# Pacing the density of the last image but one, with one product on ScalarE and its sum on GpSimd

## The chip, the core and the metric

The kernel runs on one core of a Trainium2 chip. A core has five engines with instruction queues of their own, each worked off in order: TensorE (PE: matrix products; its weight loads are listed as PEld), VectorE (DVE: elementwise work and reductions), ScalarE (ACT: activation functions with a scale and a bias), GpSimd (POOL) and SyncE (SP: here only DMA issues). The metric is the device time of one execution in microseconds (us), as the median of several runs.

## The reference

The input x has 8 images of 192 channels and 64 x 64 points. Two layers follow each other:

```
x = x + attention(group_norm(x))
x = x + density(group_norm(x))

attention: q = prelu(w1 x), k = prelu(w2 x) (24 channels), v = prelu(wa x) (192 channels)
           out = softmax(q' k over 4096 points) v
density:   l = xr - 0.5 and l = xr + 0.5, each through four small layers per channel:
             l = softplus(m_i) l + b_i          (1 -> 3 -> 3 -> 3 -> 1 values)
             l = l + tanh(f_i) * tanh(l)        (not after the last)
           likelihood = max(|sigmoid(s upper) - sigmoid(s lower)|, 1e-6), s = -sign(lower + upper)
```

So attention is matrix work and one exp per score, and the density is a long chain of products, sums and tanhs on every point, once for the lower and once for the upper side.

## The kernel before, in words

**Steps.** The attention is worked off in steps: per image 8 rows of queries (512 each), per row 16 steps (`STEPS`), so 128 steps per image (`IMG`) and 1024 in all (`last`). In step t PE makes the scores of step t + 1 (line 896, two matmuls), the scores for the row maximum of step t + 25 (line 825, `LEAD` = 25), and the products of step t with the values (line 912, eight matmuls). ScalarE takes the exp (line 901), DVE the row maximum (line 833). The last 25 steps have no maximum to make. At the end of a row, ScalarE scales the sums (line 936), PE turns them (line 946), DVE adds them to x (line 957) and takes the norm's statistics (line 516). Beside this the next image's norm, keys and values are prepared; the last image (number 7) has none of that. The row maximum has one PSUM buffer (`ps_mx`), the scores for the exp one (`ps_sc`), and exp's result two.

**Units.** The density of image b starts when its attention is done, so it runs beside the attention of image b + 1, and image 7's runs alone behind the last step (the tail). It is cut into 12 units per image: a half of the points (c), a third of the channels (g), and a side (s, lower or upper). A unit works on tiles of 128 x 1024 from a pool of 17 buffers. For the images 0 to 6 a unit is, in its written order:
- ScalarE: three first tanhs (line 1158, `tanh0`); three products of the first of them by a scale (line 1167, `begin`), to each of which GpSimd issues a DMA that adds x (line 1172);
- DVE: six products with sum (line 1186 through `mix`), two for each of the three layer values, namely with the second and with the third first tanh; behind each pair ScalarE's second tanh (line 1180);
- DVE: three gates, then six operations for the next layer, with a third round of tanhs on ScalarE, three gates, and one operation for the last layer; the last product of that layer is already made on ScalarE (line 1222, `plain`) and summed by GpSimd in two halves (line 1228).

Image 7's units make their first layer on PE: `product` (line 1125) sums x and three tanhs in PSUM for each of the three values, with a bank filled by ScalarE (line 1109, `fill`) where one was used before; ScalarE takes the tanh from there (line 1134) and DVE the first gate (line 1144).

**Endings.** When both sides of a pair are done, `ending` makes the likelihood. Where it begins before step `last - 12` the sum, difference and product go to GpSimd as pieces of half a tile (lines 1416, 1429, 1437); from there on, `alone` makes them on DVE (lines 1449, 1464, 1465). The store into x is DVE's (line 1479) in both.

**GpSimd's pieces.** A queue, `pieces`, gives out one piece per step (`pool_step`), each behind a small memset (line 1377, `pause`) that waits for the last DVE operation but one of the density, so that the piece lies beside the row maximum, which reads PSUM.

**The planner.** The order on each engine is written at build time. A step's fixed work and what is due (`due`, `run_due`) come first, then `density_step` lets units give out operations as long as they have credit. DVE's credit per step is a rate: the operations left in this image, times their cost, over the steps until a due step, plus 0.1, at most 3.1 (`MOST`). The due step is b * 128 + 271 for image b's density, and step 1032 within the last 25 steps, with a cap of 4.1 there. `Unit.step` takes an operation only if what it needs was given out in an earlier step (for DVE, only tanhs and the DMA's sums have to be earlier), if buffers are left, and if the step's cost stays below `FULL`. Behind the last step `tail_step` takes over: it keeps a clock per engine, gives each operation a duration, and gives out the one that could start first. Nothing at run time looks at these costs; only the order is left, with its waits.

`zs`, `bufs`, `norms` (scales and biases of the image's norm), `xc` (the image being added to) and `at(t, fn, cost...)` (run fn in step t) are used by all of them.

Of the kernel before, what the change touches and what calls it, by code (L numbers as in the profile page):

```python
# [11 lines left out]
AF = mybir.ActivationFunctionType  # L12
# [6 lines left out]
def kernel(  # L19
# [35 lines left out]
    F = 512  # L55
# [336 lines left out]
    def at(t, fn, cost=0.0, act=0.0, pe=0.0):  # L392

        due.setdefault(max(t, now[0]), []).append((fn, cost, act, pe))
# [617 lines left out]
            banks.append(t)  # L1012
    zs = {}

    class Unit:

        def __init__(self, b, c, g, s):
            self.key = b, c, g, s  # L1020
            self.at = {}
            self.done = {}
            self.buf = {}
            self.todo = {"DVE": deque(), "ACT": deque(), "PE": deque()}
            self.left = {"l": 6, "t": 9, "u": 0, "z": 1, "p": 1}
            self.held = {"l": 0, "t": 0, "u": 0, "z": 0, "p": 0}
            self.on_pe = b == B - 1
            add = self.add
            if self.on_pe:

                self.left.update(t=3, u=3, p=0)
                for i in range(3):
                    add("ACT", ("u", 0, i), [], self.tanh0, makes="u")
                for i in range(3):
                    after = [("u", 0, j) for j in range(3)]
                    if i:

                        add("ACT", ("fill", i), [("sum", 0)], self.fill)
                        after.append(("fill", i))
                    add(  # L1040
                        "PE", ("sum", i), after, self.product,
                        frees=[("u", 0, j) for j in range(3)] if i == 2 else [],
                    )
                    if i:
                        add("ACT", ("l", 1, i - 1), [("sum", i - 1)], self.tanh1, makes="l")
                add("ACT", ("l", 1, 2), [("sum", 2)], self.tanh1, makes="l")
                for i in range(3):
                    add("DVE", ("gate", 1, i), [("l", 1, i)], self.gate1)
            else:
                for i in range(3):  # L1050
                    add("ACT", ("t", 0, i), [], self.tanh0, makes="t")
                    if i == 0:
                        for k in range(3):
                            add(
                                "ACT", ("l", 1, k), [("t", 0, 0)], self.begin, makes="l",
                                frees=[("t", 0, 0)] if k == 2 else [],
                            )
                for i in range(3):
                    for j in (1, 2):
                        add(  # L1060
                            "DVE", ("mix", i, j), [("t", 0, j), ("x", i)], self.mix,
                            frees=[("t", 0, j)] if i == 2 else [],
                        )
                    add("ACT", ("t", 1, i), [("mix", i, 2)], self.tanh, makes="t")
                for i in range(3):
                    add("DVE", ("gate", 1, i), [("t", 1, i)], self.gate, frees=[("t", 1, i)])
            for i in range(3):
                add("DVE", ("l", 2, i), [("gate", 1, 1)], self.two, makes="l")
                add("DVE", ("add", 2, i), [("gate", 1, 2), ("gate", 1, 1)], self.third)
# [93 lines left out]
        def begin(self, k):  # L1163
            b, c, g, s = self.key
            i = k[2]
            dst, x_ = self.buf[k], self.src()
            nc.scalar.activation(  # L1167
                dst, self.buf["t", 0, 0], AF.Copy, scale=norms[b, 1][1][:, g, 3 * i : 3 * i + 1]
            )

            def add():
                nc.gpsimd.dma_start(out=dst, in_=x_, accum_op=ALU.add)  # L1172
                self.at["x", i] = now[0] + 1

            at(now[0] + 1, add)

        def tanh(self, k):
            b, c, g, s = self.key
# [113 lines left out]
        def step(self, eng, t, older):  # L1292
            todo = self.todo[eng]
            while todo and credit[eng] > 0:
                name, after, fn, makes, frees = todo[0]
                if any(self.at.get(a, t) >= t for a in after if eng != "DVE" or a[0] in "tux"):
                    return
                if makes and len(bufs) <= sum(u.need() for u in older) + len(endings):
                    return
                cost = COST[eng]  # L1300
                if spent[eng] + cost > FULL[eng] - max(0.0, late[eng] - 0.7):
                    return
                todo.popleft()
# [31 lines left out]
    def density_step(t, rate):  # L1335
        if t >= last:
            return tail_step(t)
        if units:

            left = sum(len(u.todo["DVE"]) for u in units if u.key[0] == units[0].key[0])  # L1340
            rate = left * COST["DVE"] / max(1, (units[0].key[0] + 2) * IMG + 15 - t) + OTHER
            rate = min(rate, MOST)
            if t + LEAD >= last:

                rate = min(left * COST["DVE"] / (last + 8 - t) + OTHER, MOST + 1.0)

        for eng, most in (("DVE", rate), ("ACT", ACT_RATE)):
            credit[eng] = min(credit[eng] + most, most + 1.3)
        for eng in ("ACT", "DVE"):
            order = list(range(min(3, len(units))))  # L1350
            if len(units) == 2:

                order.sort(key=lambda n: -len(units[n].todo["DVE"]))
            for n in order:
                units[n].step(eng, t, list(units)[:n])
        for u in [u for u in units if not u.busy()]:
            units.remove(u)
# [345 lines left out]
```

## Time and profile before

| | |
|---|---|
| median of 3 runs | 4351.46 us (4350.76 to 4351.48) |
| the profiled execution | 4350.1 us, span 4348.1 us |
| granted TensorE clock | 0.986 |
| PE, DVE, ACT, POOL busy | 4217.4, 3883.2, 2848.1, 1118.2 us |
| end of the last step (last L912) | 4050.0 us from the span's start |
| image 6's rows of steps, image 7's rows | 499.1, 461.2 us |

The page gives the busy time of each engine, the chain of work that ended last, and the costliest groups of instructions, each with its line, engine, operation, tiles (out<-in, buffer numbers left out), count, busy time, mean duration and the idle time ahead of it. The windows view gives, for each stretch of the span, the busy time of each engine in us with the number of its instructions, the granted clock, and the share and rate of the DMA engines. The timeline lists instructions in the order of time with their start, duration, and in brackets the engine's idle time before and what ended it; equal ones that follow each other are merged (x3). Starts are us from the span's start. A DVE operation's duration overlaps the next one's start by some 0.1 us, so the distance of starts is what one costs.

### The profile page before, as it was taken

Reading aid. Unit: us, or ns where it says so; the run is one execution under the profiler, and the core shown is the slowest. Engines: PE = TensorE matmul, PEld = TensorE weight load, DVE = VectorE, ACT = ScalarE, POOL = GpSimd, SP = SyncE. Lnnn points to the kernel's source line nnn. Section 1 sums busy time; section 2 is a strip of 40 time slices with the busy share of each in tenths; the row PEclk is TensorE's granted clock in tenths of the full one; section 3 lists DMA queues with packets and bytes.
Section 4 is the critical chain, followed back from the end, with each engine's and each line's share of the span. In section 5 each row is a group of like instructions: output and inputs, shape, how many; then the busy total and the mean of one; then the engine's idle time right before and its main releaser. Section 6 shows DMA issues by size and latency. Waiting matters only on the chain.

```text
span 4348.1 us, 59628 instructions
## 1 busy us (share of the span) xinstructions
PE 4217.4 (97%) x23464; PEld 3810.4 (88%) x23464; DVE 3883.2 (89%) x4055; ACT 2848.1 (66%) x3104; POOL 1118.2 (26%) x1204
## 2 busy tenths in 40 slices
PE   7999999999999999999999999999999999999796
PEld 4999999999999999999999999999999998999432
DVE  5444359999999998999999999999999999999999
ACT  1333337776777767677677767777677767778775
POOL 1000001432223322342233322243133323333100
PEclk7999999999999999999999999999999999999898
DMA  3201133245343444336333442435333442324100
GB/s 80 43 26 42 37 73 71 67 83 98 76 83 75 93 97 83 64 65 118 80 87 67 86 108 62 88 76 105 83 82 71 87 92 52 70 48 73 25 15 15
DMA packets 239113, 309.55 MB, mean 71 GB/s; under 512 B 91249, under 2 KB 164849, under 8 KB 238833
## 3 DMA queue, kind: packets, MB, share of 16 engines
q1 hardware_dynamic: 201472, 173.15, 17.9%
q0 software_dynamic: 36288, 132.14, 17.3%
q8 instruction: 184, 3.01, 0.3%
q14 instruction: 97, 0.79, 0.1%
q10 hardware_dynamic: 1072, 0.47, 0.1%
HBM read 131.34 MB, written 42.21 MB: 40 GB/s over the span
## 4 chain that ended last, share of the span: by engine, by line
PE 55%; DVE 35%; ACT 4%; issue 3%; DMA 2%; POOL 1%; SPq 0%; DVEq 0%; POOLq 0%; ACTq 0%
PE b L912 37%; DVE d L1186 20%; DVE rm L833 9%; PE sc L896 7%; PE mx L825 7%; PE b L786 2%; DVE st L516 2%; PE b L669 1%; ACT e L901 1%; DMA xi<-in_x_dram 1%; DVE d L1144 1%; DVE xc L957 1%; DVE v L800 1%; DVE v L795 1%; DMA nd<-rn 0%
## 5 line engine op out<-in xcount | busy, mean ns | idle before, releaser
L912 PE MATMUL b<-v,e 128*128 128x193 f32 x16384 | 2844.8, 327 | 0.0
L912 PEld LDWEIGHTS b<-v,e 128*128 128x128 f32 x16384 | 2729.6, 190 | 90.7
L901 ACT ACTIVATE e<-sc 128x1024 f32<-128x1024 f32 x1024 | 1044.8, 1020 | 1198.4 <-PE sc L896 1194.2
L833 DVE TENSOR_REDUCE rm<-mx 128x1 f32<-128x1024 f32 x999 | 1216.2, 1217 | 369.9 <-PE mx L825 369.2
L1186 DVE SCALAR_TENSOR_TENSOR d<-d,un,d 128x1024 f32<-128x1024 f32 x1008 | 1302.2, 1312 | 14.7 <-ACT d L1180 8.8
L1186 DVE SCALAR_TENSOR_TENSOR d<-d,rt,d 128x1024 f32<-128x1024 f32 x684 | 875.7, 1293 | 6.6 <-PE b L1125 0.8
L896 PE MATMUL sc<-q,kr 98*128 98x512 f32 x2048 | 781.1, 462 | 12.3 <-ACT e L901 9.5
L1180 ACT ACTIVATE d<-d,bn,wn 128x1024 f32<-128x1024 f32 x504 | 617.7, 1235 | 69.5 <-DVE d L1186 68.8
L825 PE MATMUL mx<-kr,q 96*128 96x512 f32 x1998 | 637.3, 400 | 18.4 <-DVE rm L833 17.1
L1172 POOL DMA_DIRECT2D d<-xc x252 | 220.1, 906 | 1231.1 <-ACT d L1167 977.9
L825 PEld LDWEIGHTS mx<-kr,q 96*128 96x128 f32 x1998 | 370.2, 189 | 134.4 <-DVE rm L833 50.7
L1377 POOL MEMSET pause<- 128x1 f32 x456 | 61.6, 135 | 1313.6 <-DVE d L1186 1313.5
L896 PEld LDWEIGHTS sc<-q,kr 98*128 98x128 f32 x2048 | 355.1, 191 | 39.0 <-ACT e L901 20.2
L1158 ACT ACTIVATE d<-xc,bn,wn 128x1024 f32<-128x1024 f32 x288 | 349.9, 1232 | 7.6 <-DVE bn L582 7.6
L1228 POOL TENSOR_TENSOR d<-d,d 128x512 f32<-128x512 f32 x168 | 325.7, 1940 | 39.5 <-ACT d L1222 38.2
L1167 ACT ACTIVATE d<-d,un 128x1024 f32<-128x1024 f32 x252 | 282.2, 1141 | 0.0
L695 POOL TENSOR_TENSOR kq<-kq,kh 128x256 f32<-128x256 f32 x64 | 85.3, 1333 | 380.3 <-ACT kh L690 379.7
L1429 POOL TENSOR_TENSOR d<-d,d 128x512 f32<-128x512 f32 x80 | 161.0, 2012 | 0.0
L1437 POOL TENSOR_TENSOR d<-d,d 128x512 f32<-128x512 f32 x80 | 158.2, 1977 | 1.6
L1416 POOL TENSOR_TENSOR d<-d,d 128x512 f32<-128x512 f32 x80 | 152.2, 1903 | 0.0
L1421 ACT ACTIVATE d<-d,bn,wn 128x512 f32<-128x512 f32 x160 | 121.4, 808 | 39.9 <-POOL d L1416 32.1
L786 PE MATMUL b<-wv,xi 64*128 64x192 f32 x1344 | 124.4, 331 | 0.6 <-DVE v L795 0.4
(196 smaller groups left out, 2156.8 us busy)
## 6 DMA issues: line engine op xcount, KB each, us to landing
d<-xc POOLq DMA_DIRECT2D x252, 512.0 KB, 5.4
xi<-in_x_dram SPq DMA_DIRECT2D x280, 192.0 KB
kr<-kqd SPq DMA_DIRECT2D x352, 96.0 KB
xc<-in_x_dram SPq DMA_DIRECT2D x64, 384.0 KB
out_dram<-xc SPq DMA_DIRECT2D x94, 256.0 KB
q<-kqd SPq DMA_DIRECT2D x128, 96.0 KB
kqd<-kh SPq DMA_DIRECT2D x64, 128.0 KB
kqd<-kq SPq DMA_DIRECT2D x64, 128.0 KB
```

The costliest lines, as they stand in the source:

```text
L786: nc.tensor.matmul(pv[:, s, k, :], lhsT=t[p, g, k * 128 : k * 128 + 128], rhs=wf["v", b][p, g, :], start=g == 0 and k == 0, stop=g == 2, s ...
L825: nc.tensor.matmul(sc[:, s, :], lhsT=tile_of(qt[b, n // 2], n, j)[0 : 4 * CR].bitcast(F32R), rhs=keys_of(b, c)[0 : 4 * CR, s, :].bitcast(F ...
L833: nc.vector.tensor_reduce(out=rowmax[b, n][:, j, k : k + 1], in_=sc, axis=AX.XY, op=ALU.max)
L896: nc.tensor.matmul(sc[:, s, :], lhsT=keys_of(b, ORDER[p // 4])[r, s, k : k + 128].bitcast(F32R), rhs=qt[b, n // 2][r, :, u : u + 256].bitc ...
L901: return lambda: nc.scalar.activation(e, sc, AF.Exp)
L912: nc.tensor.matmul(a[:, j, 0 : C + 1], lhsT=e[:, s, j * 128 : j * 128 + 128], rhs=v[:, s, p % 4, :], start=p == 0 and s == 0 and j % 2 == ...
L1158: nc.scalar.activation(self.buf[k], self.src(), AF.Tanh, bias=bn[:, s, g, i : i + 1], scale=wn[:, g, i : i + 1],)
L1167: nc.scalar.activation(dst, self.buf["t", 0, 0], AF.Copy, scale=norms[b, 1][1][:, g, 3 * i : 3 * i + 1])
L1172: nc.gpsimd.dma_start(out=dst, in_=x_, accum_op=ALU.add)
L1180: nc.scalar.activation(self.buf[k], self.buf["l", n, k[2]], AF.Tanh, bias=norms[b, 1][2][:, s, g, i : i + 1], scale=self.scales()[0][:, g, ...
L1186: recent.append(nc.vector.scalar_tensor_tensor(dst, src, factor, dst if plus is None else plus, ALU.mult, ALU.add))
L1228: return nc.gpsimd.tensor_tensor(z[:, n], z[:, n], dst[:, n], ALU.add)
```

## The change

For the images 0 to 5 the written order of the six products changes: the three with the second tanh come first, then the three with the third; their second tanhs are listed behind them. For image 6 (`b == B - 2`) the third value's second product leaves DVE: ScalarE multiplies the third first tanh by its scale into a buffer of its own (`beside`, kind "q"), and GpSimd adds that to the layer's value in two halves, as pieces; the second tanh of that value waits for this sum. The last DVE product of the third tanh comes after that ScalarE product, since it gives the tanh's buffer back.

The due step becomes b * 128 + 268 for the images 0 to 5 and `last - 6` (1018) for image 6 over the whole of its steps, not only the last 25; the cap in the last 25 steps stays at 4.1 and the one before at 3.1. In `Unit.step` a DVE operation's need of a "q" has to be from an earlier step too.

```diff
+    ASIDE = (()), (2,)
...
+            aside = ASIDE[b == B - 2]
...
-            self.left = {"l": 6, "t": 9, "u": 0, "z": 1, "p": 1}
+            self.left = {"l": 6, "t": 9, "u": 0, "z": 1, "p": 1, "q": len(aside)}
...
+                for i in aside:
+                    add("ACT", ("q", 1, i), [("t", 0, 2), ("x", i)], self.beside, makes="q")
                 for i in range(3):
-                    for j in (1, 2):
+                    add(
+                        "DVE", ("mix", i, 1), [("t", 0, 1), ("x", i)], self.mix,
+                        frees=[("t", 0, 1)] if i == 2 else [],
+                    )
+                for i in range(3):
+                    if i not in aside:
+                        done = i == 2 - len(aside)
                         add(
-                            "DVE", ("mix", i, j), [("t", 0, j), ("x", i)], self.mix,
-                            frees=[("t", 0, j)] if i == 2 else [],
+                            "DVE", ("mix", i, 2),
+                            [("t", 0, 2)] + [("q", 1, k) for k in aside] * done, self.mix,
+                            frees=[("t", 0, 2)] * done,
                         )
-                    add("ACT", ("t", 1, i), [("mix", i, 2)], self.tanh, makes="t")
+                for i in range(3):
+                    add(
+                        "ACT", ("t", 1, i),
+                        [("mix", i, 1), ("s", i)] if i in aside else [("mix", i, 2)],
+                        self.tanh, makes="t",
+                    )
...
+        def beside(self, k):
+            b, c, g, s = self.key
+            i = k[2]
+            src, dst = self.buf[k], self.buf["l", 1, i]
+            nc.scalar.activation(
+                src, self.buf["t", 0, 2], AF.Copy,
+                scale=norms[b, 1][1][:, g, 3 * i + 2 : 3 * i + 3],
+            )
+
+            def add(h):
+                n = slice(h * F, h * F + F)
+                if h == 1:
+                    self.at["s", i] = now[0]
+                    at(now[0] + 1, lambda: self.give(k))
+                return nc.gpsimd.tensor_tensor(dst[:, n], dst[:, n], src[:, n], ALU.add)
+
+            pieces.append(lambda: add(0))
+            pieces.append(lambda: add(1))
...
-                if any(self.at.get(a, t) >= t for a in after if eng != "DVE" or a[0] in "tux"):
+                if any(self.at.get(a, t) >= t for a in after if eng != "DVE" or a[0] in "tuxq"):
...
-            rate = left * COST["DVE"] / max(1, (units[0].key[0] + 2) * IMG + 15 - t) + OTHER
-            rate = min(rate, MOST)
-            if t + LEAD >= last:
-
-                rate = min(left * COST["DVE"] / (last + 8 - t) + OTHER, MOST + 1.0)
+            b = units[0].key[0]
+            until = (b + 2) * IMG + 12 if b < B - 2 else last - 6
+            rate = left * COST["DVE"] / max(1, until - t) + OTHER
+            rate = min(rate, MOST + (t + LEAD >= last))
```

More of the change, by code (lines that the diff above doesn't have):

```diff
@@ L1024, in __init__ @@
             self.todo = {"DVE": deque(), "ACT": deque(), "PE": deque()}
-            self.left = {"l": 6, "t": 9, "u": 0, "z": 1, "p": 1}
-            self.held = {"l": 0, "t": 0, "u": 0, "z": 0, "p": 0}
+            self.left = {"l": 6, "t": 9, "u": 0, "z": 1, "p": 1, "q": len(aside)}
+            self.held = {"l": 0, "t": 0, "u": 0, "z": 0, "p": 0, "q": 0}
             self.on_pe = b == B - 1
@@ L1029, in __init__ @@
             if self.on_pe:
-                self.left.update(t=3, u=3, p=0)
+                self.left.update(t=3, u=3, p=0, q=0)
                 for i in range(3):
```

## The prediction

> **What bounds the kernel now.** I read the totals and the chain first, then the last image row by row, then the tail. The page's totals and its chain:
>
> ```profile
> PE 4217.4 (97%) x23464; PEld 3810.4 (88%) x23464; DVE 3883.2 (89%) x4055; ACT 2848.1 (66%) x3104; POOL 1118.2 (26%) x1204
> ...
> PE 55%; DVE 35%; ACT 4%; issue 3%; DMA 2%; POOL 1%; SPq 0%; DVEq 0%; POOLq 0%; ACTq 0%
> ```
>
> TensorE (PE) and VectorE (DVE) share the path, so work taken from DVE pays only where DVE is the later one. To see where, I cut the windows view at every 16th exp (L901), one row of 16 steps each. These are the eight rows of the last image, image 7; image 6's density runs beside them.
>
> ```profile
> core 0: us, PE busy (x) PEld busy (x) DVE busy (x) ACT busy (x) POOL busy (x), PEclk, DMA share, GB/s
> 3588.80:3649.70 60.90, 59.23 (x330) 54.16 (x328) 58.90 (x71) 43.20 (x47) 17.67 (x19) 1.00 0.15 31
> 3649.70:3708.80 59.10, 57.75 (x322) 54.17 (x323) 57.90 (x52) 50.91 (x54) 30.29 (x32) 1.00 0.53 94
> 3708.80:3768.50 59.70, 58.60 (x334) 55.07 (x333) 58.11 (x57) 39.53 (x42) 16.94 (x19) 1.00 0.32 56
> 3768.50:3826.00 57.50, 57.50 (x328) 54.60 (x327) 55.57 (x54) 42.66 (x44) 16.29 (x17) 1.00 0.31 61
> 3826.00:3884.10 58.10, 57.78 (x328) 54.55 (x327) 56.88 (x54) 42.85 (x46) 19.17 (x18) 1.00 0.34 48
> 3884.10:3941.70 57.60, 57.34 (x322) 53.86 (x321) 55.35 (x51) 47.31 (x52) 26.30 (x26) 1.00 0.46 76
> 3941.70:3997.20 55.50, 55.13 (x318) 52.11 (x317) 48.46 (x47) 42.23 (x56) 13.47 (x17) 1.00 0.28 46
> 3997.20:4050.00 52.80, 52.60 (x308) 50.34 (x306) 47.09 (x42) 47.99 (x58) 14.21 (x16) 1.00 0.36 71
> ```
>
> A row that PE sets takes 57.5 us: row 3 has no idle PE, and rows 5 and 6 of image 0, where DVE is busy only 22 us, take 57.5 too. Rows 0, 1, 2 and 4 are longer and are DVE's busy time plus 1.2 to 2.0 us: DVE sets them. From step 999 on no row maximum is left (LEAD is 25), and DVE idles 12.7 of the 82.8 us to the end of the last step at 4050.0, called E below. After E the tail is DVE's: busy 50.9 of the first 53.4 us and 233.5 of the last 244.7. So DVE work is free in the last row and a half, dear in the tail, and close to dear before.
>
> **The prices.** DVE's density operation and the two helpers:
>
> ```profile
> L1186 DVE SCALAR_TENSOR_TENSOR d<-d,un,d 128x1024 f32<-128x1024 f32 x1008 | 1302.2, 1312 | 14.7 <-ACT d L1180 8.8
> L1186 DVE SCALAR_TENSOR_TENSOR d<-d,rt,d 128x1024 f32<-128x1024 f32 x684 | 875.7, 1293 | 6.6 <-PE b L1125 0.8
> ...
> L1228 POOL TENSOR_TENSOR d<-d,d 128x512 f32<-128x512 f32 x168 | 325.7, 1940 | 39.5 <-ACT d L1222 38.2
> ...
> L1167 ACT ACTIVATE d<-d,un 128x1024 f32<-128x1024 f32 x252 | 282.2, 1141 | 0.0
> ```
>
> Back to back, L1186 starts every 1.2 us (x3 in 3.67), so 1.2 is what one operation costs DVE. A product moved aside costs ScalarE 1.14 us and GpSimd two halves of 1.94 us.
>
> **Part 1, one product aside.** Image 6 has 12 units, so 12 DVE operations go: 14.4 us of DVE. Added are 12 x 1.14 = 13.7 us on ScalarE, idle 104 us in these eight rows, and 24 GpSimd halves. These are not free for DVE. In DVE's timeline 44 of the L1186 operations took over 1.6 us, together 45.7 us too much, and each lay beside a GpSimd sum, 21 of them also beside a DMA issue:
>
> ```profile
> 3741.90 0.87 POOL L1172 DMA_DIRECT2D d<-xc  x1
> ...
> 3742.12 3.08 DVE L1186 SCALAR_TENSOR_TENSOR d<-d,un,d 128x1024 f32<-128x1024 f32 x1
> ...
> 3742.54 1.57 POOL L1228 TENSOR_TENSOR d<-d,d 128x512 f32<-128x512 f32 x1
> ```
>
> Spread over the 408 halves of the density that is 0.11 us a half; 24 cost DVE 2.7 us. Bounds: 0, and 24 x 1.8 (the example's excess) = 43. I take 0.11, the mean of the same instruction, since each added half also waits for a DVE operation and starts beside the maximum.
>
> [...]
>
> **Part 2, order and pace.** All images but the last get their three first products ahead of the three second ones, and the due time comes three steps earlier (b*128 + 268 for 271). Per image the planner places about 228 operations in both; before step 896 it has placed 7 more than now. Where PE sets the row they are free; the other end is 7 x 1.2 = +8.4 us. Going through the rows of images 1 to 6 with the larger of PE's floor (image 0: 58.0, 59.6, 66.0, 64.8, 61.3, 57.5, 57.5, 66.8) and DVE's busy time changed by 1.2 an operation gives +2.0, +0.5, -1.8 and three times -0.8: **-1.7**, say -1.5, with -8 and +8.4 as bounds. The new order of the mixes moves no wait that I can see: L1186's idle is 21 us in the whole run.
>
> In image 7 the planner places, by row, 30, 28, 28, 28, 28, 29, 27, 31 operations now and 23, 27, 31, 32, 29, 30, 27, 30 then; GpSimd pieces go from 60 to 85 (24 halves and six of the last but one ending, less five of image 5's, done earlier). With 1.2 us an operation, 0.11 a piece, DVE's busy time plus 1.2 and the floor of 57.5 (58.5 in row 0, which carries the norm):
> - row 0: 60.9 to 58.5, -2.4; row 1: 56.7 + 1.2, -1.2
> - row 2: 58.1 + 3.6 + 0.7 + 1.2 = 63.6, +3.9; row 3: 55.6 + 4.8 + 0.4 + 1.2 = 62.0, +4.5
> - row 4: 56.9 + 1.2 + 0.7 + 1.2 = 60.0, +1.9; row 5: +0.4
> - rows 6 and 7: 14 to 9 operations in the seven steps that still have maxima, -0.6; the rest hidden, as DVE idles 12.7 us there.
>
> Sum **+6.5**. With -1.5, E comes 5.0 us later.
>
> **Part 3, the tail.** Image 6 leaves 10 operations behind the last step for 29 now, and its last but one ending, now at E, takes L1464 and L1465 to GpSimd and its store (L1479) ahead of E: 19 + 3 operations of 1.2, 26 us less DVE work. But now this work covers the start of image 7's density:
>
> ```profile
> 4060.52 1.21 DVE L1186 SCALAR_TENSOR_TENSOR d<-d,rt,d 128x1024 f32<-128x1024 f32 x1
> ...
> 4066.39 0.16 DVE L564 RECIPROCAL rq<-sq 128x1 f32<-128x1 f32 x1
> ...
> 4094.71 1.27 DVE L1144 SCALAR_TENSOR_TENSOR d<-d,si,b 128x1024 f32<-128x1024 f32 x1
> ...
> 4098.29 1.28 DVE L1144 SCALAR_TENSOR_TENSOR d<-d,si,b 128x1024 f32<-128x1024 f32 x1
> ...
> 4102.21 1.27 DVE L1144 SCALAR_TENSOR_TENSOR d<-d,si,sc_tail 128x1024 f32<-128x1024 f32 x1
> 4103.41 3.79 DVE L1186 SCALAR_TENSOR_TENSOR d<-d,rt,d 128x1024 f32<-128x1024 f32 x3
> ```
>
> The first unit's third gate ends and its mixing begins at 4103.4, E + 53.4. What is late next when the cover goes is PE: a sum takes 6.87 us (sums start at 4077.58, 4084.45, 4091.31) and the first unit's third is, in the new order, the fourth. Up to the norm's reciprocal DVE is filled as now (five operations for four), so it comes only 0.5 us earlier. The third tanh of image 7 then follows at E + 23.0 for 24.85 now (a tanh of image 6 goes from ahead of it), and the first sum ends at E + 25.9. The second sum wants tanhs that stand on ScalarE behind three of image 6's ending, and those wait for two GpSimd halves: its end is E + 32 (34.4 now), and 6.87 each to the fourth: E + 45.8. A tanh (1.2) and a gate (1.2) make 48.4 for 53.4: **-5.0**. From there DVE is busy throughout, as now, with four operations less (L1464, L1465 and L1479 of image 6, and one gate done early): **-4.9**. Bounds: -26 if cover were not needed; -4 if the fourth sum comes as late as E + 47 and DVE waits some 3 us more further on.
>
> **Sum**: +5.0 - 5.0 - 4.9 = -4.9. The profiled execution took 4350.1 (span 4348.1), 1.4 under the median; from it 4345.2, and against the median of 4351.46 it is **4346.6**.
>
> **Rivals.**
> 1. *PE hides the moved work.* Rows 2 to 4 stay near 59: DVE may lag inside a row and catch up where it idles, as it does in the last 25 steps. For it: row 3 has 1.9 us of idle DVE, rows 6 and 7 have 12.7. Against it: DVE is busy 97% in row 2 and the reduce of each step frees the one buffer PE waits for. The +10.3 of rows 2 to 4 shrinks to about +2: -4.9 - 8.3 = -13, 4338.
> 2. *ScalarE waits for GpSimd, slower.* The third tanh of each unit now waits for a sum on GpSimd, and behind it on ScalarE stands the next step's exp, which PE waits for. Place: 12 tanhs of image 6. Waits of this sort exist (L1421 on L1416 32.1 us in 37, longest 2.1) and PE's own waits for exp (L896 on L901) are 9.5 us in the whole run, so now they are nearly all covered. With 2.0 us of stall a unit it costs 24: +19, 4370; it decides (beyond +8.7) from 1.1 us a unit.
> 3. *The change doesn't do what it says.* Ten operations of image 6 still stand behind the last step, 13 steps late rather than six early. If the tail then starts as late as now, only the -4.9 stays and E's +5.0 takes it back: 4351.
>
> **How the numbers follow.** Forecast 0.43 (own range 4343 to 4352), rival 1 0.37, rival 2 0.14, rival 3 0.06. About 0.2%, 8.7 us, is what a measurement of this kernel can tell from no change: faster 0.37, within it 0.43 + 0.06 = 0.49, slower 0.14. The range reaches from rival 1's 4338 less 1.5 to the forecast with E 10 us later than I take it, 4357; most of rival 2 is left out.
>
> **What would show it.** Right: rows 2 and 3 of image 7 at 61 us or more, row 0 near 58; the first L1144 within 36 us of E and the first mixing of image 7 at E + 48; DVE idle some 20 us between E + 16 and E + 48. Wrong: rows 2 to 4 at 58 (rival 1); PE's waits for exp above 20 us and ScalarE's third tanh waiting for the new sum (rival 2); mixing at E + 53 (rival 3).

## The result, and the profile after

The changed kernel takes **4360.67 us** (median of 20 runs, 4357.55 to 4362.78) beside 4351.77 for the kernel before in the same series (20 runs). The ratio is 1.0019 with an interval of 1.0013 to 1.0025; in a later series it was 1.0018 (1.0009 to 1.0026). So the change makes the kernel some 8 us slower. The prediction had 4346.6, 4.9 us less than before, and the time is 3.7 us above its range. By the bound of 0.2% it lies just inside "no change"; the sign of the forecast is wrong.

The profiled execution has a span of 4357.1 us for 4348.1. Totals and chain of the page:

```profile
PE 4215.2 (97%) x23472; PEld 3810.6 (87%) x23472; DVE 3870.7 (89%) x4040; ACT 2858.3 (66%) x3117; POOL 1159.0 (27%) x1264
...
PE 68%; DVE 26%; issue 2%; ACT 1%; DMA 1%; POOL 1%; SPq 0%; DVEq 0%; POOLq 0%; ACTq 0%
```

DVE lost 12.5 us of work, GpSimd gained 41, and the kernel became longer: the totals cannot tell why. E, the end of the last step, comes at 4066.3 for 4050.0, so 16.3 later where 5.0 was predicted. The tail behind it takes 290.8 for 298.1, so 7.3 less where 9.9 was predicted. Of the 16.3, 14.8 come from image 7's rows, 0.6 from the images 1 to 6 together, and 0.9 from what precedes them. The eight rows of image 7, cut as in the prediction:

```profile
core 0: us, PE busy (x) PEld busy (x) DVE busy (x) ACT busy (x) POOL busy (x), PEclk, DMA share, GB/s
3590.28:3652.82 62.54, 58.93 (x330) 54.44 (x330) 59.37 (x70) 37.12 (x40) 11.24 (x13) 1.00 0.06 13
3652.82:3711.95 59.13, 57.39 (x322) 53.55 (x321) 49.33 (x45) 48.01 (x50) 27.82 (x31) 1.00 0.50 103
3711.95:3774.82 62.87, 59.54 (x334) 54.62 (x333) 62.70 (x61) 48.88 (x51) 30.03 (x31) 1.00 0.32 45
3774.82:3838.49 63.67, 60.24 (x334) 55.20 (x333) 62.62 (x58) 48.01 (x52) 25.30 (x27) 1.00 0.32 65
3838.49:3897.36 58.87, 57.31 (x326) 53.98 (x325) 57.87 (x55) 45.41 (x49) 27.49 (x30) 1.00 0.28 54
3897.36:3958.49 61.13, 58.11 (x324) 53.48 (x323) 60.92 (x54) 49.60 (x54) 28.82 (x28) 1.00 0.42 70
3958.49:4012.27 53.78, 53.78 (x312) 51.62 (x312) 47.21 (x48) 47.06 (x61) 23.26 (x27) 1.00 0.48 69
4012.27:4066.30 54.03, 53.42 (x307) 49.99 (x305) 47.48 (x36) 47.25 (x59) 25.52 (x27) 1.00 0.19 40
```

Rows 2, 3 and 5 are DVE's, as long as DVE is busy plus 0.2 to 1.1. But look at row 1: DVE is idle for 9.8 us, and the row is still 59.1, as long as before, and 1.6 over PE's floor. Row 0 became 1.6 us longer, too. The timeline of DVE shows what a row's sum hides. From the start of row 1:

```profile
3653.29 1.23 DVE L833 TENSOR_REDUCE rm<-mx 128x1 f32<-128x1024 f32 x1 [2.33 <-PE mx L825]
3656.84 1.23 DVE L833 TENSOR_REDUCE rm<-mx 128x1 f32<-128x1024 f32 x1 [2.33 <-PE mx L825]
...
3660.40 1.22 DVE L833 TENSOR_REDUCE rm<-mx 128x1 f32<-128x1024 f32 x1 [2.24 <-PE mx L825]
3661.54 2.47 DVE L1222 SCALAR_TENSOR_TENSOR d<-d,un,d 128x1024 f32<-128x1024 f32 x2
3663.95 1.22 DVE L833 TENSOR_REDUCE rm<-mx 128x1 f32<-128x1024 f32 x1
```

from row 0, DVE and then PE:

```profile
3606.01 1.22 DVE L833 TENSOR_REDUCE rm<-mx 128x1 f32<-128x1024 f32 x1
3607.14 4.99 DVE L1222 SCALAR_TENSOR_TENSOR d<-d,rt,d 128x1024 f32<-128x1024 f32 x4
3612.05 1.22 DVE L833 TENSOR_REDUCE rm<-mx 128x1 f32<-128x1024 f32 x1
...
3613.32 0.73 PE L825 MATMUL mx<-kr,q 96*128 96x512 f32 x2 [1.32 <-DVE rm L833]
```

and from row 3:

```profile
3784.75 3.00 DVE L1222 SCALAR_TENSOR_TENSOR d<-d,un,d 128x1024 f32<-128x1024 f32 x2
3787.68 1.21 DVE L833 TENSOR_REDUCE rm<-mx 128x1 f32<-128x1024 f32 x1
3788.82 3.66 DVE L1222 SCALAR_TENSOR_TENSOR d<-d,un,d 128x1024 f32<-128x1024 f32 x3
3792.40 1.21 DVE L833 TENSOR_REDUCE rm<-mx 128x1 f32<-128x1024 f32 x1
```

The maxima (L833) are 3.55 us apart where PE sets the step. Into that go one maximum (1.13 from start to start) and **two** density operations (2.4), as from 3660.40 to 3663.95. A step with none is no shorter here: DVE waits 2.33 us for PE's next scores. A step with three takes DVE 4.72 (3787.68 to 3792.40), one with four 6.04 (3606.01 to 3612.05). Since the maximum has one PSUM buffer, PE then waits for DVE, as the 1.32 us at 3613.32 show. So where DVE has no time to spare, a third operation costs 1.2 us, and one missing elsewhere gives nothing back. Shorter steps lie mostly behind long ones, where DVE catches up: of the 15 under 3.4 us in rows 0 to 6 of the changed kernel, 13 come within three steps behind one of over 4.2 (the one right behind the 6.04 took 3.19). In image 7 the number of density operations between two maxima went from 0 (5 steps), 1 (22), 2 (67), 3 (10) to 0 (11), 1 (22), 2 (52), 3 (18), 4 (1). Steps longer than 4.2 us went from 14 to 30, and what they take over 3.55 from 17.5 to 37.4 us. Their neighbours count as well: before, 6 of the 10 steps of three were followed by a step of at most one operation that took less than 3.4 us (2.6 to 3.2), so the lag was made up; in the changed kernel that is so behind 4 of the 19 steps of three or four. The waits of DVE and PE for each other in rows 0 to 6 of the kernel before, and in rows 0 to 6 of the changed one (us in total, times, longest):

```profile
DVE rm L833 <- PE mx L825: 8.3, 13, 1.1
...
PE mx L825 <- DVE rm L833: 2.6, 5, 0.9
```

```profile
DVE rm L833 <- PE mx L825: 17.7, 10, 2.8
...
PE mx L825 <- DVE rm L833: 14.2, 15, 2.1
```

Both waits grew. A shift of work from one engine to another would be expected to lengthen one and shorten the other; steps that became uneven lengthen both.

### The profile page after: what moved, and what is told of

Same layout as the page of the kernel before. It is cut to its first block, busy times and chain, and to the rows that moved or that the text cites. A ratio compares the mean times of both kernels' runs of the same rounds, so it can differ in the third digit from the quotient of the medians.

```text
span 4357.1 us, 59716 instructions
## 1 busy us (share of the span) xinstructions
PE 4215.2 (97%) x23472; PEld 3810.6 (87%) x23472; DVE 3870.7 (89%) x4040; ACT 2858.3 (66%) x3117; POOL 1159.0 (27%) x1264
## 3 DMA queue, kind: packets, MB, share of 16 engines
q1 hardware_dynamic: 201472, 173.15, 17.5%
## 4 chain that ended last, share of the span: by engine, by line
PE 68%; DVE 26%; issue 2%; ACT 1%; DMA 1%; POOL 1%; SPq 0%; DVEq 0%; POOLq 0%; ACTq 0%
PE b L912 45%; DVE d L1222 16%; PE sc L896 9%; PE mx L825 8%; DVE rm L833 6%; PE b L786 3%; PE b L669 2%; DVE d L1161 1%; PE b L946 1%; DMA xi<-in_x_dram 1%; DVE xc L1514 0%; DVE st L516 0%; DVE v L800 0%; PE b L1142 0%; POOL d L1451 0%
## 5 line engine op out<-in xcount | busy, mean ns | idle before, releaser
L833 DVE TENSOR_REDUCE rm<-mx 128x1 f32<-128x1024 f32 x999 | 1216.9, 1218 | 382.0 <-PE mx L825 380.6
L1222 DVE SCALAR_TENSOR_TENSOR d<-d,un,d 128x1024 f32<-128x1024 f32 x996 | 1288.4, 1322 | 9.1 <-DMA d<-xc 6.2
L695 POOL TENSOR_TENSOR kq<-kq,kh 128x256 f32<-128x256 f32 x64 | 75.6, 1182 | 382.2 <-ACT kh L690 381.9
```

Of the source, the lines that this page charges most:

```text
L833: nc.vector.tensor_reduce(out=rowmax[b, n][:, j, k : k + 1], in_=sc, axis=AX.XY, op=ALU.max)
L1222: recent.append(nc.vector.scalar_tensor_tensor(dst, src, factor, dst if plus is None else plus, ALU.mult, ALU.add))
```

## The experiments

Times are ratios to the kernel before on the same chip, with their 95% interval; 0.0010 is 4.4 us. Rows, E and tail are from each run's profile. Two traces of the changed kernel, from the first series and from the last below, differ by 7.0 us, of which 6.3 lie ahead of image 3's rows and none in image 7's; so rows and tails of image 7 can be compared between runs, the total span less well. "Change" is the kernel as changed, "aside" the product on ScalarE with its sum on GpSimd.

### Which part costs: pace, aside, order

Pacing with the new order, no aside (`ASIDE = (), ()`):

> The changed kernel without the product aside (all six products on VectorE in image 6, in the new order), with its new due steps. 201 large VectorE operations stand behind the last step, as in the changed kernel (202; before 224), so 12 more of them fall into image 7's rows. Theory 'rows': what was moved ahead of the last step stretches rows that VectorE already set, 1.2 us an operation: the last step ends 10 to 15 us later than in the changed kernel (4066), the tail stays near 291, total +10 to +15 against the changed kernel, +19 to +24 against before. Rival 'helpers': the loss comes from the 12 products on ScalarE and the 24 sums on GpSimd (longer VectorE operations beside them, waits of ScalarE and of the DMA issues); then this one is faster than the changed kernel by 5 to 10, at or below before +4.

Aside and new order with the old due steps (the old lines of `rate`):

> The changed kernel with the due steps of before (b*128 + 271, step 1032 in the last 25 steps), so order and product aside alone. 220 large VectorE operations behind the last step (224 before). Theory 'rows': image 7's rows lose some 8 operations, the last step ends 5 to 9 us earlier than before (4050), the tail is 4 operations shorter (-5): -5 to -12 against before. Rival 'helpers': the sums and products cost more than the 14.4 us of VectorE work that they save: +3 to +10 against before. Rival 'order': the same, since the order alone costs it (see the run with the order alone).

The new order alone (both edits above):

> The new order of the products and second tanhs alone: nothing aside, due steps of before. Theory 'rows': the work and its place hardly change: within 3 us of before. Rival 'order': the three second tanhs come bunched behind the products and gates follow too soon, so VectorE waits for ScalarE: +6 or more, with L1186's idle behind ScalarE above 20 us in image 7's rows.

The change with the images 0 to 5 at their old due step:

```diff
-            until = (b + 2) * IMG + 12 if b < B - 2 else last - 6
+            until = (b + 2) * IMG + 15 if b < B - 2 else last - 6
```

> The changed kernel with the due step of the images 0 to 5 put back to b*128 + 271; image 6 is due at 1018 and has its product aside as in the change. Theory 'rows': image 5 hands some 7 operations over into image 7's first row, which VectorE sets, so the last step ends 0 to 8 us later than in the changed kernel; 208 operations are left behind it for 202, +7: total +3 to +12 against the changed kernel. Rival 'earlier images': the pace of the images 0 to 5 is what costs (their rows are 2 us longer in sum); then -2 to -4 against the changed kernel.

Measured: pace 1.0002 (0.9993 to 1.0010), aside and order 1.0035 (1.0023 to 1.0048), order alone 1.0031 (1.0020 to 1.0043), change with the old due step 1.0034 (1.0022 to 1.0046). Without the aside the kernel is 7 us faster than the change: the theory 'rows', 10 to 15 us slower, is refuted, and the rival 'helpers' gave the number. With the old due steps its rival 'order' came: the loss of 15 us is that of the order alone, within 2 us. The change with the old due step lies in the range of 'rows' (7 us slower), but not for its reason: image 7 takes 469.6 us for 476.0, and the images 3 to 6 are 17 us longer. The order alone costs 14 us at the old due step, on the images 3 to 6 (498 to 500 us each before, 502.5 to 505.1 with it): what the prediction held to move no wait. It is not ScalarE's tanhs that DVE waits for (3.1 us in the run). Summed over the images 3 to 6, the rows 5 and 7 are 14.5 us longer, with DVE 11.4 us busier there; rows 1, 3 and 4 have 20.7 us less DVE work and are 0.9 us longer together; rows 0, 2 and 6 have 13.1 us more and are 2.7 longer. So operations moved from rows where their absence gives nothing back to rows where DVE sets the time; that this is all of the 14 us is argued, not shown. With the due step three earlier, as in the change, the images 1 to 6 together are as before.

### Collision, due step, cap

The 24 halves of the new sum cut to 2 columns, so the third layer value lacks most of its last product:

```diff
                     at(now[0] + 1, lambda: self.give(k))
+                n = slice(h * F, h * F + 2)
                 return nc.gpsimd.tensor_tensor(dst[:, n], dst[:, n], src[:, n], ALU.add)
```

> The changed kernel in its own written order and with all its waits, but each of the 24 added GpSimd sums adds 2 columns in place of 512, so the rest of those sums is left out of the computation. What the sums' own time costs comes off. Theory 'sums collide' (VectorE's operations beside them are longer, ScalarE's tanh and the DMA issues on GpSimd's queue wait for them): image 7's rows and the tail get shorter by 4 to 9, total -4 to -9 against the changed kernel. Theory 'steps' (what costs is how many VectorE operations stand between two row maxima: with three or more VectorE sets the step, and a step with none gives nothing back): the order is the same, so within 3 us of the changed kernel.

The kernel before with due step 268 for the images 0 to 5:

> Before, with only the due step of the images 0 to 5 at b*128 + 268 for 271: order of the products, image 6's pace and all else as before. Theory 'steps': in the written order, images 3 to 6 have 11 to 14 steps with three or more density operations between two maxima for 20 before, so these images' rows get 1 to 3 us shorter each, image 7 about as before (12 steps without any for 6, 11 with three or more for 14): -4 to -12 against before. Theory 'rows' (the prediction's: operations per row count, and these are the same): within 3 us of before. Rival 'earlier due is what costs': +3 or more.

The change with a cap, in image 7's steps that have a maximum, of two density operations a step (`given` starts as `[-1, 0]`):

```diff
+                if eng == "DVE" and last - IMG <= t < last - LEAD:
+                    if given[0] == t and given[1] >= 2:
+                        return
+                    given[:] = t, given[1] * (given[0] == t) + 1
```

> The changed kernel, with at most two density operations a step on VectorE in image 7's steps that still have a row maximum (2 steps with three or more between two maxima in the written order, 21 without the cap). 216 large operations stand behind the last step for 202. Theory 'steps': image 7's rows fall from 476 to 462 to 467, the tail grows by up to 14 x 1.2: between -8 and +3 against the changed kernel, with the last step at 4053 to 4058. Theory 'rows': VectorE's load of the rows falls by about 9 operations, the last step comes 5 to 9 earlier and the tail takes 14 x 1.2 = 17 more: +5 to +12. Rival 'sums collide': the last step comes less than 5 earlier, as the 24 sums stay.

The kernel before with that cap in all steps that have a maximum:

> Before, with at most two density operations a step on VectorE in all steps that have a row maximum; order, pace and helpers as before. In the written order no gap between two maxima holds three or more (20 per image before), 22 hold one for 37; 221 large operations stand behind the last step for 224. Theory 'steps': every image from 1 on gets 3 to 8 us shorter, -20 to -45 against before. Theory 'rows': the same operations per row, within 4 us of before.

Measured: small sums 1.0004 (0.9996 to 1.0013), some 6 us less than the change, as the theory 'sums collide' had it. Long density operations (over 1.6 us) in image 7 go from 14 with 12.4 us too much to 7 with 5.3. So the sums do cost DVE, about 0.25 us a half; against the run without the aside, which has 8 with 8.7, it is 0.16. The due step alone gives 0.9988 (0.9979 to 0.9997): -5, within the range of its theory 'steps'. Where these 5 us lie is not shown: its images 3 to 7 and its tail are together as long as before, where the theory had 1 to 3 us less in each of the images 3 to 6. The cap gives 0.9990 (0.9981 to 0.9999): 12 us less than the change, and the changed kernel's rows 1 to 5 become

```profile
3657.20:3714.03 56.83, 56.83 (x322) 53.95 (x321) 48.26 (x42) 44.63 (x48) 22.48 (x28) 1.00 0.50 98
3714.03:3773.50 59.47, 58.65 (x334) 55.15 (x333) 57.27 (x58) 44.82 (x47) 25.02 (x26) 1.00 0.32 47
3773.50:3831.00 57.50, 57.50 (x328) 54.60 (x327) 56.13 (x53) 45.20 (x46) 25.78 (x27) 1.00 0.25 47
3831.00:3889.01 58.01, 57.74 (x328) 54.54 (x327) 56.50 (x55) 45.82 (x49) 28.82 (x28) 1.00 0.34 62
3889.01:3946.22 57.21, 57.10 (x322) 53.79 (x321) 54.74 (x50) 49.08 (x53) 30.77 (x30) 1.00 0.40 79
```

Row 3 is back at 57.50 with no idle PE, and image 7 takes 463.5 for 476.0. PE's wait for the maximum falls from 14.2 to 0.3 us. The theory had not let the cap win that much, since 14 more operations stand behind E (216 for 202 of all large ones); but the tail is as long as the change's (290.7), with DVE idle 16.5 us of it for 32.2, so they lie in its idle time. In the kernel before the cap gives nothing, 0.9999 (0.9991 to 1.0008), where 'steps' expected 20 to 45 us and 'rows' none: PE waits for maxima only 1 to 3 us an image there, and 1 to 4 with the cap. That expectation took long steps for lost time; by these waits the lag of most was made up before PE met it.

### With the old order

Old order, no aside, due steps 268 and 1018, cap in image 7 (the cap's lines as above; `ASIDE = (), ()`, and the written order of before where nothing is aside):

```diff
+                if not aside:
+                    for i in range(3):
+                        for j in (1, 2):
+                            add(
+                                "DVE", ("mix", i, j), [("t", 0, j), ("x", i)], self.mix,
+                                frees=[("t", 0, j)] if i == 2 else [],
+                            )
+                        add("ACT", ("t", 1, i), [("mix", i, 2)], self.tanh, makes="t")
+                else:
...
```

> Old order of the products in all images, nothing aside; the change's due steps (b*128 + 268, and 1018 for image 6), and at most two density operations a step in image 7's steps with a row maximum. Theory 'steps in image 7, order in the others, sums that cost their own time': images 1 to 6 as in the run with the due step alone (some 2990 us together), image 7 460 to 464, tail 287 to 293: -8 to -16 against before, and below all runs so far. Rival 'the product aside is what made the tail short': the tail is near 298, -3 to +3.

The same with the aside in image 6, in the changed order there (`ASIDE = (()), (2,)`):

> The run with old order, pace and cap, plus the product aside in image 6 alone (image 6 in the changed order, the others in the old one). Theory: the 24 sums cost what the 12 products save: +0 to +7 against the run without it, tail within 3 us of it. Rival 'aside pays once the steps are capped': 4 or more below it.

The first of these with image 6's old due step (the old lines of `rate`, `+ 12` for the images 0 to 5):

> The run with old order, pace and cap, with image 6's due steps of before (1039, then 1032): 222 large operations behind the last step for 215. Theory 'cover': the operations that stay behind the last step lie in the tail's idle time, but the early part of the tail is then theirs: tail 296 to 300, image 7 457 to 460, total -4 to -9 against before, 2 to 8 above the run with the new pace. Rival 'pace of image 6 gains nothing': within 2 us of it.

The second with the aside only for the first half of the points (`ASIDE[b == B - 2 and c == 0]`):

> As the run with the product aside, but only for the six units of the first half of the points; these end before the last 25 steps, which have no row maximum for a GpSimd sum to lie beside. Theory 'sums collide where no maximum is': within 2 us of the run without aside. Rival 'each sum costs the same': half of the difference between the runs with and without aside.

Measured: 0.9988 (0.9980 to 0.9997), 0.9976 (0.9967 to 0.9985), 0.9989 (0.9980 to 0.9997), 0.9976 (0.9966 to 0.9985). The second is 7 us faster than the first, against its theory (the tail is 290.7 for 294.1, with DVE idle 16.5 us of it for 20.3, and image 7 takes 461.5 for 465.4). But it differs from the first by two things, the aside and the new order in image 6, and the next section shows which of them it is. The first stayed short of its -8 to -16. Under the cap and in the old order, pacing image 6 gains nothing, as the rival of the third said. The fourth missed both its theories: six units aside do what twelve do. **The second and the fourth beat both kernels**, by 10 to 12 us against before and some 19 against the change (medians 4345.35 and 4344.95, with 4356.82 for before there).

### What was still open

Of the two kernels with aside and without in the old order, the cap's lines taken out (f1, f3); of the capped change, the aside (`ASIDE = (), ()`, f2); and the cap, as `t < last - LEAD` in all images, put on the new order alone (f4):

> The changed kernel with one thing undone: the images 0 to 5 have their old order of the six products (due step 268, image 6 aside and paced as in the change, no cap). If the new order costs only at the due step 271 and the aside costs through bunched steps, this is as slow as the changed kernel: 1.0013 to 1.0025, image 7 near 474, the images 1 to 6 within 5 us of it. If the new order is what the change loses (the rival from the comparison of the capped kernels, where the old order stood each time that the aside paid), it is near 0.9985, some 15 us less than the changed kernel, with the images 1 to 6 some 10 us shorter.

> The changed kernel with the cap of two density operations a step in image 7, and without the aside (its order and pacing stay). With the cap and the aside it took 0.999 of before. If the aside pays once steps are capped, whatever the order, this is 5 to 8 us slower than that: 1.0002 to 1.0009, with E about as early and the tail 4 to 8 us longer, since the twelve products more lie behind E. If the aside pays only with the old order, it is 0.999 or less.

> Pacing alone: the old order in all images, no aside, no cap, due steps 268 and 1018. The old order with due step 268 alone took 0.9988. If pacing image 6 to step 1018 costs by putting more operations into image 7's steps than its maxima leave room for, this is 1.0000 to 1.0010, with image 7 at 470 to 475 us and steps of three and more operations in its rows 2 to 5. If that pacing is harmless without the aside and the new order, it is 0.9985 to 0.9992 with image 7 near 462.

> The kernel before with the new order of the six products alone (1.0031 with nothing else), and the cap of two density operations in every step that has a row maximum. If the new order costs at the due step 271 because it bunches the operations (three and four in a step, others without), the cap gives it back: 0.9995 to 1.0010, with the images 3 to 6 back at 498 to 501 us each. If it costs by waits of the order itself (VectorE waiting for a tanh or GpSimd's DMA), the cap does not help: 1.0025 or more.

Measured: 1.0005 (0.9996 to 1.0013), 0.9986 (0.9977 to 0.9995), 0.9998 (0.9989 to 1.0007), 1.0086 (1.0072 to 1.0099). The first is between its two theories: the order costs the change some 6 us, not 15, and image 7 still takes 474.8. The second came as its rival said: on the same chip the capped change took 4351.67 with the aside and 4350.41 without, so under the cap the aside pays nothing. Its image 7 and tail together take 752.4 us with image 6 in the new order and nothing aside. The run with old order in the others, new order in image 6 and the aside takes 752.2 there, the one with the old order throughout and nothing aside 759.5. So the 7 us above are those of image 6's order under the cap, and not of the aside; old order in the others, new order in image 6 and nothing aside, which would show it alone, was not run. In the third, image 7 takes 474.3 without aside and in the old order, with 16 steps of three operations, where the run with the due step alone has 459.3: the pace of image 6 alone bunches it. The fourth lies in the range of "the cap does not help", but not for the reason given there. Capped, the order took some 36 us more than before; 20 of that is a new wait, seen in PE's waits:

```profile
PE mx L826 <- DMA kr<-kqd: 22.1, 4, 10.0
...
PE mx L826 <- DVE rm L834: 16.2, 24, 1.6
```

Twice PE stands 9 to 10 us for the next image's keys (kr), a wait that the kernel before does not have. So it says nothing on bunching as the order's mechanism.

The change and the pace alone, on one chip:

> The changed kernel itself, beside the next one on one chip, since the kernel before differed by some 5 us between the chips of this study (4351.8 and 4356.7 to 4357.0). If the change costs the same everywhere, 1.0013 to 1.0025 again; if chips weigh it differently, about 1.0005, as the nearest kernel (old order, no cap) had on another chip.

> The changed kernel without the aside (new order and pacing stay), on the same chip as the run above. If the aside costs 7 us where steps are not capped, this is 7 us less than that run (0.9985 less of its ratio, within 2 us). If the aside's cost was a difference of chips, the two are within 3 us, as with the old order (0.0007 apart there).

Measured: 1.0018 (1.0009 to 1.0026) and 1.0001 (0.9992 to 1.0010), medians 4365.44 and 4357.51. The aside costs the change 7 to 8 us; it is not a difference of chips. Of this the two traces place 4.4 us in the tail (291.0 for 286.6) and 1.2 in image 7's rows (476.0 for 474.8); the rest they do not place.

The runs add up as a chain from the kernel before, each link by the ratios (each ratio is good to about 4 us, so a link of 2 us is not clear of the noise):
- due step 268 for the images 0 to 5: 0.9988, **-5.2**
- image 6 paced to step 1018: 0.9998, **+4.4**; by the traces image 7's rows lose 15.0 and the tail wins 10.1
- the new order: 1.0002, **+1.7** (with the aside it is some 6, as the first of the four runs under "What was still open" shows)
- the aside: 1.0019, **+7.4**; of it some 6 the sums on GpSimd (1.0004 with small ones)

## Why the prediction was wrong

The forecast was the sum of four parts, -1.5, +6.5, -5.0 and -4.9. In the profiles they are +0.6, +14.8, -0.4 and -6.9, and 0.9 lie ahead of them.

**What bounds the kernel**: right as far as it went. A row that PE sets takes 57.5, and the capped kernel's row 3 is that again.

**Image 7's rows (+6.5; measured +14.8): the step that failed.** It took each row as the larger of PE's floor and "DVE's busy time plus 1.2". Rows 2 and 3 came as said (62.9 and 63.7 for 63.6 and 62.0), and rival 1, that PE hides the moved work, is refuted by them and by PE's 14.2 us of waits. But rows 0 and 1 were to win 3.6 and lost 1.7: fewer operations do not make rows shorter when they stand three or four to a step beside empty steps. Row 5 took 61.1 for 58.0. The numbers of operations were right: cut at the maxima, the trace has the planner's 23, 27, 31, 32, 29 and 30 in rows 0 to 5, and there row 1 takes 60.5 for 57.0 before, with one operation less. The sum had to look at the steps. A price of 1.2 for each operation beyond two gives +12.0 (24.0 for 12.0 before), nearer to 14.8 than 6.5 is; but it is no rule, since it also gives 12 to the cap in the kernel before, where image 7 won 2.4 and the kernel nothing. What a long step costs depends on whether the next ones leave room. The cap, which changes that distribution and little else, takes 12.5 us off image 7; and the aside is not needed for the loss, as the pace alone brings it (474.3 for 459.3).

**The price of a half beside DVE (0.11; measured 0.16 to 0.3).** The mean over all halves was too low for these. Against the run with small sums, the 24 sums cost some 6 us by time and 7.1 by the long operations of image 7, against the run without the aside 3.8 by these, for 2.7 predicted; the bounds, 0 and 43, held. The 0.11 was a mean over halves of which most (313 of 408) come second and wait themselves (last section).

**Images 1 to 6 (-1.5; measured +0.6).** "The new order of the mixes moves no wait that I can see" failed: it looked at DVE's waits, while the order moved operations between steps and rows. The small net is a gain of some 5 us from the due step and a loss from the order that is 14 us at the old one. Why the order puts them there stays open; the run that should have told it brought a wait for the keys instead.

**The start of the tail (-5.0; measured -0.4).** The first gate came at E + 35.8, as said (within 36). But the first mixing of image 7 starts at 4119.34, E + 53.0, for E + 48.4:

```profile
4102.11 1.28 DVE L1161 SCALAR_TENSOR_TENSOR d<-d,si,b 128x1024 f32<-128x1024 f32 x1 [1.00 <-ACT d L1151]
4104.47 1.28 DVE L1161 SCALAR_TENSOR_TENSOR d<-d,si,b 128x1024 f32<-128x1024 f32 x1 [1.07 <-ACT d L1151]
4111.28 1.28 DVE L1161 SCALAR_TENSOR_TENSOR d<-d,si,sc_tail 128x1024 f32<-128x1024 f32 x1 [5.53 <-ACT d L1151]
```

The spacing of PE's sums, 6.87 us, is as predicted. (The prediction's own terms, 45.8 + 1.2 + 1.2, make 48.2 and not 48.4.) What failed is that the norm's reciprocal comes "0.5 us earlier": it comes at E + 18.6 for 16.4. So PE's first sum ends at E + 30.0 for 25.9, and the fourth at 50.6 for 45.8.

The aside is what makes it late. In the run without it (the pace alone, the last one above) the reciprocal comes at E + 14.5 and the first mixing at E + 48.0 (48.8 in the same kernel's other run), as predicted; with the small sums it is 16.7 and 50.8. Without the aside DVE waits for PE at E; in the change it is 2.9 us late there. First that run, then the change, DVE and GpSimd:

```profile
4058.26 1.22 DVE L1514 SCALAR_TENSOR_TENSOR xc<-d,xc 128x1024 f32<-128x1024 f32 x1
...
4074.37 0.18 DVE L932 RECIPROCAL rc<-b 128x4 f32<-128x4 f32 x1 [1.36 <-PE b L912]
```

```profile
4053.54 2.30 DVE L1514 SCALAR_TENSOR_TENSOR xc<-d,xc 128x1024 f32<-128x1024 f32 x1
4055.76 4.80 DVE L1222 SCALAR_TENSOR_TENSOR d<-d,rt,d 128x1024 f32<-128x1024 f32 x3
...
4069.23 0.17 DVE L932 RECIPROCAL rc<-b 128x4 f32<-128x4 f32 x1
```

```profile
4052.60 2.16 POOL L1208 TENSOR_TENSOR d<-d,d 128x512 f32<-128x512 f32 x1
...
4054.76 2.21 POOL L1208 TENSOR_TENSOR d<-d,d 128x512 f32<-128x512 f32 x1
```

Two of the moved sums (L1208) run here beside DVE, where no maximum is left to lie beside; the store and the first of the three products take 2.3 us each for 1.2. With the small sums they take 1.2 to 1.3, and DVE is 1.0 us late. So about half of the delay is the sums' own time. What makes the other half stays open. DVE also idles 6.2 us for x in the last row, in rows where the prediction called DVE work free; but with small sums it idles 5.8 there, so the moved sums do not hold that up, and without the aside it idles as long in all for other things (3.3, 1.5 and 1.4 us). In the last row 8 density operations are long, by 7.4 us in all; without the aside 5, by 4.6; before 1, by 1.0.

**The rest of the tail (-4.9; measured -6.9)** came near: behind the first mixing it takes 237.8 us for 244.7, 2.0 less than said, and no run shows why.

**Rival 2**, ScalarE waiting for GpSimd, had the sign and not the mechanism: PE's waits for exp stay at 2.2 us in rows 0 to 6. **Rival 3**: its sign, mixing at E + 53, came, but not for its reason, as the work did move ahead of E (204 large operations stand behind it for 224). The case that happened, bunched steps in image 7 and sums that make DVE late at E, was not among them.

## What to carry to other kernels

Where two engines meet once per step through one buffer, look at the steps and not at the row: here an operation too many could cost its whole 1.2 us (4.72 for a step of three, 3.55 where PE sets the step), one too few elsewhere gave nothing back (3.55 with none, with DVE idle 2.33 of it), and a mean of busy time shows neither. Long steps alone were no loss, though: where they cost, PE waited for the maximum (14.2 us in image 7 of the change, 0.3 with the cap; 2.6 before). A cap on what one step may take took 12 us off the change, and nothing off the kernel before. And when two things are added together, as the aside and image 6's order were here, a run with each alone is needed to tell which one paid: the aside cost 7 us in the change and paid nothing under the cap.

## What the runs showed of the hardware

How DVE and GpSimd meet was not expected so clear. Take the density operations (and others of their form) of the trace before that have no DMA issue beside them. The 39 that start while a GpSimd half is running with over 0.1 us still to go take 1.79 us in the mean, 22 of them over 1.6; the 287 in which a half starts only later take 1.28, none over 1.6; the 1334 that meet none take 1.26. The halves pay the other way round: 2.13 us where a DVE operation runs at their start (313), 1.33 where none meets them (43). In the changed kernel it is 1.78 (60), 1.27 (311) and 1.26 (1308), and 2.12 and 1.43. Who comes first goes on (1.28 us for the 287), and the other ends a nearly constant time behind it: of the 39, the 36 of 128 x 1024 all end 1.08 to 1.09 us after the half that they met, and of the 313 halves 304 end 1.12 to 1.16 us after the operation that they met. By these times the second waits for all of the first; that makes the 39 longer by 0.5 us in the mean (1.79 for 1.26) and the 313 halves by 0.8 (2.13 for 1.33). So it is the halves already running when DVE's operation comes that cost.

Beside a GpSimd DMA issue it is worse: where a half starts during a DVE operation that has an issue beside it, the operation takes 1.87 us (22, of which 7 over 1.6) in place of 1.28 (287); in the changed kernel 2.43 (16). Why is not shown. Issues without a half cost nothing (1.27, 179).

The kernel before took 4351.8 us in the first series and 4356.7 to 4357.5 on the four chips of the later ones, which is as much as most effects here, so the runs are compared by ratios on one chip.
